# A two-layer decoder on one Trainium2 core: the last attention's value products turned round, with softmax sums on VectorE

## The chip, the cores and the metric

The kernel runs on one core of a Trainium2 chip. The metric is the device time of one execution in microseconds (us): lower is better. The core has a matrix engine (TensorE, in the profile PE, its weight loads PEld), a vector engine (VectorE, DVE), a scalar engine (ScalarE, ACT), a general engine (GpSimd, POOL) and a queue engine that here only issues transfers (SyncE, SP). Matrix products land in PSUM, eight banks of 128 partitions by 512 float32; everything else is in SBUF or in DRAM.

## The reference, cut to what matters

A batch of 32 sequences of 56 tokens with 128 features goes through two post-norm layers. Each has self-mixing, cross attention on a context of 1500 rows by 128 features per sequence, and a mixture of eight experts. The change touches the cross attention of layer 1:

```
q  = layernorm(x) @ w_q               # 16 heads of 64
k, v = split(context @ w_kv)          # 16 heads of 64
scores = einsum('bqhd,bkhd->bhqk', q * 64**-0.5, k)
attn = softmax(scores, axis=-1)       # over 1500 context rows
out = einsum('bhqk,bkhd->bqhd', attn, v)
return (out @ w_out + b_out) * tanh(gate)
```

The kernel folds the key projection into the queries and the value projection into the output weights, so that scores and values are both products with the context itself: for each sequence there are 16 x 56 = 896 query columns of 128 features.

## The kernel before, in words

All arithmetic is float32. The work of layer 1's cross attention is written by the generator `attention()` (L1059). It goes over 64 blocks: for each of the 32 sequences one of 512 query columns and one of 384 (`BLOCKS`). The 1500 context rows are cut into 12 chunks (`CK`) of 125 rows (`PK`). A pass of its loop writes three things that overlap:

- the scores of the current block `cur`. For each chunk, one product (L1077) of the transposed context `amT` (stationary, 128x125) with the queries (moving, 128x512 or 128x384) into one of three banks of pool `p_s`, which ACT copies to the SBUF tile `s` (L1078). DVE keeps a running maximum of the chunks in `m` (L1083 to L1087).
- the values of the block before, `prev`. For each 128 query columns, 12 products (L1182) of the probabilities (stationary, 125x128) with the context rows `amN` (moving, 125x129) into one of two banks of pool `p_v`. The 129th column of `amN` is one, so the last column of the bank is the sum of the probabilities. DVE takes its reciprocal `rz` (L1189), and ACT scales the bank by it into `ao` (L1191).
- the outputs of the block before that, `old`: TensorE transposes each `ao` tile into a bank, and DVE copies it into `qo` (L1199). `outputs` stands at chunk 5 of the next score loop.

Between them stand `maxima` (TensorE transposes `m`, DVE reduces), `spread` (the negated maxima transposed back into rows, `nb`, copied by ACT at L1163), and the four parts of `probabilities` (DVE adds `nb` to three chunks, L1171; ACT takes the exponential, L1174). Some of those parts are still due when the next score loop begins.

At every `yield` of `attention()` a hand-written planner (L1279 to L1306) writes steps of two other threads into the program: `pre` (layer 0 and the first half of layer 1 for later sequences) and `post` (output projection and experts of finished sequences). Their matmuls use pool `p_f`. How many steps it writes follows from the product count of `attention()` so far, so filler and attention keep pace. The framework then decides the order on each queue: it may move a ready instruction past one that stands earlier in the code. In the profile, for example, the copy L1199, written behind a maximum at chunk 5, runs ahead of it.

All transfers are issued from SP before the change. The opening works on the first two groups of sequences in step: loads of weights, of `xin` (L967) and of contexts, then `self_attention` with the transposes of x as its first product. `obias`, a small product and an addition (L396), stands ahead of it.

Of the kernel before, what the change touches and what calls it, by code (L numbers as in the profile page):

```python
# [69 lines left out]
def decoder_kernel(  # L70
# [86 lines left out]
        clock["pe"] += TRANSPOSE  # L157


    ident = const.tile([P, P], F32, name="ident")  # L160
    make_identity(nc, ident)

    sq = const.tile([P, N_SQ], F32, name="sq")
    nc.sync.dma_start(sq[:, : 4 * D], sq_w[:, : 4 * D])
    vec = const.tile([P, N_VEC], F32, name="vec")
    nc.sync.dma_start(vec, vecs)
    row = const.tile([P, N_ROW], F32, name="row")
    nc.sync.dma_start(row, rows.to_broadcast([P, N_ROW]))
    svec = const.tile([SD, len(SVEC)], F32, name="svec")
# [18 lines left out]
    qo = [const.tile([P, 2, NQ], F32, name=f"qo{i}") for i in range(3)]  # L188

    qpad0 = const.tile([P, G, 64], F32, name="qpad")  # L190
    nc.gpsimd.memset(qpad0, 0.0)
# [14 lines left out]
    def vcol(name):  # L206
        i = VEC.index(name)
        return vec[:, i : i + 1]
# [180 lines left out]
    def ahead(a, b, tag="res", bufs=2):  # L389
# [3 lines left out]


    obias = const.tile([TP, D], F32, name="obias")
    nc.vector.tensor_tensor(  # L396
        obias, linear(vcol("bv0").to_broadcast([P, TP]), sqw("wo0"), D, TP), rowb("bo0"), ALU.add
    )

# [15 lines left out]
    def self_attention(xs):  # L415
# [8 lines left out]
            .unsqueeze(2).to_broadcast([P, nb, 2, S]),  # L424
        )
        xT = xd[:, :, 0, :]
        res = [ahead(t, obias) for t in xs]
        yield HOP
        qpad = here(qpad0, "qpad")[:, :nb]
# [565 lines left out]
    early = {}  # L995

    def opening(g):
        xs = load_x(g)
        load_x0(GROUPS[g][0])
        yield 0  # L1000
        xs = yield from self_attention(xs)
        xs = yield from cross_attention_0(xs, g)
        if g == 0:
            load_attended_T(0)
            acc = yield from experts_0(xs)
            early["weights"] = True
            yield from behind_experts(acc, g)
            return
        load_attended(0)
        while "weights" not in early:  # L1010
            yield None
        acc = yield from experts_0(xs)

        while not leader.over:
            yield None
        place["aside"] = None
        early["acc"] = []
        for a in acc:
            t = tok_tile("acc")
            nc.gpsimd.tensor_copy(t, a)  # L1020
            early["acc"].append(t)
# [34 lines left out]

    def attention():  # L1059
        blocks = [(b, q0, n) for b in range(B) for q0, n in BLOCKS]  # L1060
        prev = None
# [1 line left out]
        tail = []  # L1063
        for i in range(len(blocks) + 2):
            cur = None
            if i < len(blocks):
                b, q0, n = blocks[i]
                if q0 == 0:
# [6 lines left out]
                for c in range(CK):  # L1075
                    ps = bank(p_s, "s")
                    mm(ps[:PK, :n], amT[:, c * PK : (c + 1) * PK], qT)  # L1077
                    nc.scalar.copy(s[:, c, :], ps[:PK, :n])  # L1078


                    if c % 2 == 1 and 1 < c < CK - 2:
                        a = s[:, 0:2, :] if c == 3 else m
                        nc.vector.tensor_tensor(m, a, s[:, c - 1 : c + 1, :], ALU.max)  # L1083
                        if c == CK - 3:
                            nc.vector.tensor_tensor(m[:, 0, :], m[:, 0, :], m[:, 1, :], ALU.max)  # L1085
                    elif c >= CK - 2:
                        nc.vector.tensor_tensor(m[:, 0, :], m[:, 0, :], s[:, c, :], ALU.max)  # L1087
                    if c % 2 == 0 and tail:
                        tail.pop(0)()
                    if not tail:  # L1090
                        table["gelu"] = True
                    if c == 5 and old is not None:
                        outputs(old)
                        old = None
                    if c % 2:
                        yield 0
                if q0 and b + 1 < B:
                    load_attended_T(b + 1)
            elif old is not None:
                outputs(old)  # L1100
                old = None
            for f in tail:
                f()
            tail = []
            os = []
            nt = prev[2] // P if prev else 0
            for t in range(max(nt, 2)):
                if t < nt:
                    po = values(prev, t)
                    for k in range(3):  # L1110
                        next(po)
                        if t == 1 and k == 1 and cur:
                            table["gelu"] = False
                            nb = spread(cur, nm)
                            tail = probabilities(cur, nb)
                            for f in tail[:1]:
                                f()
                            tail = tail[1:]
                        yield 0
                    os.append(next(po))  # L1120
                elif t == 1 and cur:
                    yield 1.0
                    nb = spread(cur, nm)
                    tail = probabilities(cur, nb)
                if t == 0 and cur:
                    if not nt:
                        yield 1.0
                    nm = maxima(cur, m)
                if t >= 2 and tail:
                    tail.pop(0)()  # L1130
            if prev:
                old = (prev, os)
# [23 lines left out]
    def spread(blk, nm):  # L1156

        n = blk[2]
        ps = bank(p_t, "t")
        for t in range(n // P):  # L1160
            tr(ps[:PK, t * P : (t + 1) * P], nm[:, t : t + 1].to_broadcast([P, PK]))
        nb = mid.tile([PK, 512], F32, tag="nb", name="nb")[:, :n]
        nc.scalar.copy(nb, ps[:PK, :n])  # L1163
        return nb

# [9 lines left out]

        return [lambda k=k: part(k) for k in range(4)]

    def values(blk, t):
        b, _, _, s = blk
        po = bank(p_v, "v")  # L1180
        for c in range(CK):
            mm(  # L1182
                po[:, : D + 1], s[:, c, t * P : (t + 1) * P], amN[b % 2][:, c, :],
                start=(c == 0), stop=(c == CK - 1),
            )
            if c % 4 == 3:
                yield
        rz = tiny.tile([P, 1], F32, tag="rz1", name="rz1")
        nc.vector.reciprocal(rz, po[:, D : D + 1])  # L1189
        o = work.tile([P, D], F32, tag="ao", name="ao", bufs=5)  # L1190
        nc.scalar.activation(o, po[:, :D], AF.Copy, scale=rz)  # L1191
        yield o

    def outputs(old):
        (b, q0, n, _), os = old
        ps = bank(p_t, "t")
        for t, o in enumerate(os):
            tr(ps[:, t * P : (t + 1) * P], o)
        nc.vector.tensor_copy(qo[(b // 2) % 3][:, b % 2, q0 : q0 + n], ps[:, :n])  # L1199
        if q0 and b % 2:  # L1200
            attended.add(b // 2)

# [193 lines left out]
```

## Time and profile before

| | |
|---|---|
| median of three runs | 2210.01 us (2209.82 to 2216.82) |
| the profiled execution | 2217.4 us, its span 2215.7 us |
| PE busy | 2146.1 us, 97% of the span |
| DVE busy | 1436.4 us, 65% |
| ACT busy | 1208.6 us, 55% |
| POOL busy | 142.5 us, 6% |
| mean granted TensorE clock | 0.992 |
| mean transfer rate | 78 GB/s |

A line of a group reads: line, engine, operation, output<-inputs, shapes, how many | busy us, mean ns of one | how long the engine stood idle just before them and who ended that. PE busy is not the same as PE cost: matmuls are pipelined, so the duration of one overlaps the next. What a product costs in a stream is the distance from its start to the next one's start. Each float32 product is two matmul instructions in the trace.

### The profile page before, as it was taken

Reading aid. Unit: us, or ns where it says so; the run is one execution under the profiler, and the core shown is the slowest. Engines: PE = TensorE matmul, PEld = TensorE weight load, DVE = VectorE, ACT = ScalarE, POOL = GpSimd, SP = SyncE. Lnnn points to the kernel's source line nnn. Section 1 sums busy time; section 2 is a strip of 40 time slices with the busy share of each in tenths; the row PEclk is TensorE's granted clock in tenths of the full one; section 3 lists DMA queues with packets and bytes.
Section 4 is the critical chain, followed back from the end, with each engine's and each line's share of the span. In section 5 each row is a group of like instructions: output and inputs, shape, how many; then the busy total and the mean of one; then the engine's idle time right before and its main releaser. Section 6 shows DMA issues by size and latency. Waiting matters only on the chain.

```text
span 2215.7 us, 36884 instructions
## 1 busy us (share of the span) xinstructions
PE 2146.1 (97%) x14560; PEld 1706.4 (77%) x14560; DVE 1436.4 (65%) x2981; ACT 1208.6 (55%) x2165; POOL 142.5 (6%) x230
## 2 busy tenths in 40 slices
PE   7799999999999999999999999999999999999997
PEld 5677778778877787777877878777887878878876
DVE  4367655866577656766577765777567766667774
ACT  2455575556455556556555555555465556565551
POOL 2000001100010000100010000100001000000000
PEclk9899999999999999999999999999999999999998
DMA  7621431143211522124320343113331132111221
GB/s 200 179 81 31 112 71 62 51 125 85 75 31 57 133 84 73 31 77 116 90 64 17 93 117 97 41 30 111 102 90 29 57 106 81 43 42 50 60 79 37
DMA packets 164300, 172.17 MB, mean 78 GB/s; under 512 B 9464, under 2 KB 136864, under 8 KB 164000
## 3 DMA queue, kind: packets, MB, share of 16 engines
q1 hardware_dynamic: 164128, 169.82, 27.5%
q8 instruction: 115, 1.88, 0.4%
q14 instruction: 57, 0.47, 0.1%
HBM read 144.29 MB, written 25.49 MB: 77 GB/s over the span
## 4 chain that ended last, share of the span: by engine, by line
PE 68%; DVE 9%; ACT 3%; POOL 2%; issue 1%; DMA 1%; POOLq 0%; SPq 0%; ACTq 0%; DVEq 0%
PE f L147 25%; PE s L147 20%; PE v L147 18%; DVE s L1171 4%; PE f L156 3%; PE t L156 3%; POOL rs L360 2%; DVE m L1083 1%; ACT s L1174 1%; DVE m L1087 1%; ACT nb L1163 0%; ACT s L1078 0%; DVE st L351 0%; DMA memT<-big 0%; DVE m L1085 0%
## 5 line engine op out<-in xcount | busy, mean ns | idle before, releaser
L147 PE MATMUL v<-amN,s 125*128 125x129 f32 x5376 | 695.4, 276 | 0.9 <-ACT s L1174 0.5
L147 PEld LDWEIGHTS v<-amN,s 125*128 125x128 f32 x5376 | 655.5, 191 | 36.1 <-issue 23.5
L147 PE MATMUL s<-qo,amT 128*125 128x512 f32 (+1 forms) x1536 | 648.1, 543 | 1.9 <-ACT s L1078 1.9
L1078 ACT COPY s<-s 125x512 f32<-125x512 f32 (+1 forms) x768 | 399.7, 538 | 267.7 <-PE s L147 265.0
L1171 DVE TENSOR_TENSOR s<-s,nb 125x1536 f32<-125x1536 f32 (+1 forms) x256 | 392.9, 1545 | 59.2 <-ACT nb L1163 58.7
L147 PEld LDWEIGHTS s<-qo,amT 128*125 128x125 f32 x1536 | 264.1, 188 | 162.9 <-issue 95.2
L1174 ACT ACTIVATE s<-s 125x1536 f32<-125x1536 f32 (+1 forms) x256 | 339.1, 1328 | 85.4 <-DVE s L1171 79.9
L1083 DVE TENSOR_TENSOR m<-m,s 125x1024 f32<-125x1024 f32 (+1 forms) x192 | 208.8, 1088 | 67.6 <-ACT s L1078 65.6
L360 POOL TENSOR_TENSOR rs<-rs,mhalf 112x1 f32<-112x1 f32 x126 | 81.9, 661 | 1702.9 <-DVE rs L359 1456.0
L1191 ACT ACTIVATE ao<-v,rz 128x128 f32<-128x128 f32 x224 | 81.0, 363 | 163.8 <-DVE rz L1189 163.6
L753 ACT ACTIVATE hT<-f,vec 128x224 f32<-128x224 f32 (+1 forms) x256 | 95.3, 435 | 73.8 <-PE f L147 73.3
L147 PEld LDWEIGHTS f<-wd,hT 128*112 128x112 f32 x960 | 114.7, 180 | 16.7 <-ACT hT L753 7.3
L147 PE MATMUL f<-wd,hT 128*112 128x128 f32 x960 | 124.3, 279 | 1.7 <-ACT hT L753 1.4
L147 PE MATMUL f<-pxT,w 128*128 128x224 f32 (+1 forms) x576 | 118.1, 344 | 3.1 <-DMA w<-in_up_dram 1.4
L147 PE MATMUL f<-xT,wu 128*128 128x224 f32 (+1 forms) x512 | 110.3, 351 | 7.6 <-DMA wu<-in_wup_dram 6.4
L147 PEld LDWEIGHTS f<-pxT,w 128*128 128x128 f32 x576 | 99.0, 194 | 20.1 <-issue 4.2
L147 PEld LDWEIGHTS f<-xT,wu 128*128 128x128 f32 x512 | 90.6, 194 | 24.7 <-issue 13.2
L1083 DVE TENSOR_TENSOR m<-s 125x1024 f32<-125x1024 f32 x64 | 69.5, 1086 | 61.4 <-ACT s L1078 61.1
L771 DVE SCALAR_TENSOR_TENSOR acc<-f,wmix,acc 112x128 f32<-112x128 f32 x120 | 41.1, 347 | 86.9 <-PE f L147 86.8
L1163 ACT COPY nb<-t 125x512 f32<-125x512 f32 x64 | 34.0, 532 | 111.1 <-PE t L156 111.1
L1087 DVE TENSOR_TENSOR m<-m,s 125x384 f32<-125x384 f32 (+1 forms) x128 | 80.3, 628 | 21.2 <-ACT s L1078 14.9
L147 PE MATMUL f<-w,h 128*112 128x128 f32 x512 | 78.7, 276 | 1.6 <-DVE th L936 1.6
(289 smaller groups left out, 2376.1 us busy)
## 6 DMA issues: line engine op xcount, KB each, us to landing
amT<-memT SPq DMA_DIRECT2D x32, 750.0 KB
amN<-in_mem_dram SPq DMA_DIRECT2D x34, 672.0 KB
memT<-big SPq DMA_DIRECT2D x30, 750.0 KB
cxN<-in_mem_dram SPq DMA_DIRECT2D x30, 672.0 KB
wu<-in_wup_dram SPq DMA_DIRECT2D x72, 256.0 KB
wd<-in_wdn_dram SPq DMA_DIRECT2D x72, 256.0 KB
w<-in_gate_dram SPq DMA_DIRECT2D x72, 128.0 KB
w<-in_up_dram SPq DMA_DIRECT2D x72, 128.0 KB
```

The lines of the kernel that those rows point to most:

```text
L147: nc.tensor.matmul(ps, lhsT=lhsT, rhs=rhs, start=start, stop=stop)
L156: nc.tensor.transpose(ps, in_, ident[:k, :k])
L360: nc.gpsimd.tensor_tensor(rs, rs, mhalf[:TP], ALU.pow)
L753: nc.scalar.activation(hT[:, u0 + k, :], ps[:, k * nt : (k + 1) * nt], AF.Gelu, bias=vec[:, c : c + 1],)
L771: nc.vector.scalar_tensor_tensor(acc[j], down(last[1], last[0][1], nu, j), w[:, j, e - 1 : e], acc[j], ALU.mult, ALU.add,)
L1078: nc.scalar.copy(s[:, c, :], ps[:PK, :n])
L1083: nc.vector.tensor_tensor(m, a, s[:, c - 1 : c + 1, :], ALU.max)
L1087: nc.vector.tensor_tensor(m[:, 0, :], m[:, 0, :], s[:, c, :], ALU.max)
L1163: nc.scalar.copy(nb, ps[:PK, :n])
L1171: nc.vector.tensor_tensor(c, c, nb.unsqueeze(1).to_broadcast([PK, 3, n]), ALU.add)
L1174: nc.scalar.activation(c, c, AF.Exp)
L1191: nc.scalar.activation(o, po[:, :D], AF.Copy, scale=rz)
```

## The change

In layer 1's value products the context chunk (125x128) is now stationary and the block's probabilities (125x512 or 125x384) move, so a block takes 12 products instead of 48 or 36, and the result already has features on partitions. No transpose of an `ao` tile remains. The sums of the probabilities no longer come from a column of ones. DVE adds the chunks in pairs, five additions a block (`chunk_sums`, at chunks 2 to 10 of the next score loop). At chunk 1 of the score loop after that, eight small products with a 125x32 tile of ones finish the sums into four quarters of a `p_v` bank, and DVE takes reciprocals (`inverse_sums`). At chunk 4, ACT's queue stores one row of each quarter to DRAM (`store_sums`); at chunk 8 it loads them back, repeated on all 128 partitions (`spread_sums`); at chunk 11, DVE multiplies the value bank by them into `qo` (`outputs`). The bank of the values is held until then. The loop over values yields 12 times for every block. `maxima`, `spread` and the parts of `probabilities` move to chunks 2, 4, 8 and 11 of it.

In the opening, the first two x tiles are loaded from ACT's queue ahead of everything else, into a part of `qo`; `vecs` is loaded ahead of the first part of `sq`; and `obias` is made behind the first copy of the transposed x.

```diff
+    qo = [const.tile([P, 2, NQ], F32, name=f"qo{i}") for i in range(3)]
+    x_first = [qo[i][:TP, 0, :D] for i in range(2)]
+    for i, t in enumerate(x_first):
+        nc.scalar.dma_start(t, x[i * TP : (i + 1) * TP, :])
     ident = const.tile([P, P], F32, name="ident")
     make_identity(nc, ident)
     sq = const.tile([P, N_SQ], F32, name="sq")
-    nc.sync.dma_start(sq[:, : 4 * D], sq_w[:, : 4 * D])
     vec = const.tile([P, N_VEC], F32, name="vec")
     nc.sync.dma_start(vec, vecs)
+    nc.sync.dma_start(sq[:, : 4 * D], sq_w[:, : 4 * D])
...
+    ones = const.tile([PK, 32], F32, name="ones")
+    nc.gpsimd.memset(ones, 1.0)
...
         xT = xd[:, :, 0, :]
+        if not made:
+            make_obias()
+            made.append(True)
...
     def opening(g):
-        xs = load_x(g)
+        xs = [x_first[g]]
...
             cur = None
+            adds = chunk_sums(prev) if prev else []
...
-                    if c == 5 and old is not None:
-                        outputs(old)
-                        old = None
+                    if adds and c in (2, 4, 6, 8, 10):
+                        adds.pop(0)()
+                    if old is not None:
+                        if c == 1:
+                            old = (*old, inverse_sums(old))
+                        elif c == 4:
+                            old = (*old, store_sums(old))
+                        elif c == 8:
+                            old = (*old, spread_sums(old))
+                        elif c == CK - 1:
+                            outputs(old)
+                            old = None
...
+            if prev:
+                po = bank(p_v, "v")
+            for c in range(CK):
+                if prev:
+                    value_chunk(prev, po, c)
+                if cur and c == 2:
...
+                    nm = maxima(cur, m)
+                if cur and c == 4:
...
+                    tail.pop(0)()
+                if tail and prev and (c == 8 or c == CK - 1 and prev[2] == 512):
+                    tail.pop(0)()
+                if prev:
+                    yield 0
...
-    def values(blk, t):
...
+    def chunk_sums(blk):
+        _, _, n, s = blk
+        f = mid.tile([P, 2, 512], F32, tag="zf", name="zf")[:PK, :, :n]
+        def add(c):
+            nc.vector.tensor_tensor(
+                f, s[:, 0:2, :] if c == 2 else f, s[:, c : c + 2, :], ALU.add
+            )
+        sums[0] = f
+        return [lambda c=c: add(c) for c in range(2, CK, 2)]
+    def inverse_sums(old):
+        n, f = old[0][2] // 4, old[2]
+        ps = bank(p_v, "v")
+        for g in range(4):
+            for k in range(2):
+                mm(
+                    ps[32 * g : 32 * g + 32, :n], ones, f[:, k, g * n : (g + 1) * n],
+                    start=(k == 0), stop=(k == 1),
+                )
+        rz = work.tile([P, P], F32, tag="rz1", name="rz1", bufs=1)[:, :n]
+        nc.vector.reciprocal(rz, ps[:, :n])
+        return rz
+    def value_chunk(blk, po, c):
+        b, _, n, s = blk
+        mm(po[:, :n], amN[b % 2][:, c, :D], s[:, c, :], start=(c == 0), stop=(c == CK - 1))
+    def store_sums(old):
+        n = old[0][2] // 4
+        zd = dram.tile([4, P], F32, tag="zd", name="zd", bufs=4)[:, :n]
+        nc.scalar.dma_start(zd, old[3].rearrange("(g r) n -> g r n", g=4)[:, 0, :])
+        return zd
+    def spread_sums(old):
+        n = old[0][2]
+        rzb = mid.tile([P, 512], F32, tag="nb", name="rzb")[:, :n]
+        nc.scalar.dma_start(
+            rzb.rearrange("p (g n) -> p g n", g=4),
+            old[4].unsqueeze(0).to_broadcast([P, 4, n // 4]),
+        )
+        return rzb
     def outputs(old):
-        (b, q0, n, _), os = old
-        ps = bank(p_t, "t")
-        for t, o in enumerate(os):
-            tr(ps[:, t * P : (t + 1) * P], o)
-        nc.vector.tensor_copy(qo[(b // 2) % 3][:, b % 2, q0 : q0 + n], ps[:, :n])
+        (b, q0, n, _), po, *_, rzb = old
+        nc.vector.tensor_tensor(
+            qo[(b // 2) % 3][:, b % 2, q0 : q0 + n], po[:, :n], rzb[:, :n], ALU.mult
+        )
```

More of the change, by code (lines that the diff above doesn't have):

```diff
@@ L186, in decoder_kernel @@
     memT = [dram.tile([P, CK * PK], F32, tag=f"memT{b}", name=f"memT{b}") for b in range(B)]
-    qo = [const.tile([P, 2, NQ], F32, name=f"qo{i}") for i in range(3)]
+    ones = const.tile([PK, 32], F32, name="ones")
+    nc.gpsimd.memset(ones, 1.0)
     qpad0 = const.tile([P, G, 64], F32, name="qpad")
@@ L395, in decoder_kernel, with make_obias @@
     obias = const.tile([TP, D], F32, name="obias")
-    nc.vector.tensor_tensor(
-        obias, linear(vcol("bv0").to_broadcast([P, TP]), sqw("wo0"), D, TP), rowb("bo0"), ALU.add
-    )
+    made = []
+    def make_obias():
+        nc.vector.tensor_tensor(
+            obias, linear(vcol("bv0").to_broadcast([P, TP]), sqw("wo0"), D, TP), rowb("bo0"), ALU.add
+        )
     HOP, NORM, LOAD = 2.5, 6.0, 14.0
@@ L1099, in attention @@
             elif old is not None:
-                outputs(old)
+                old = (*old, inverse_sums(old))
+                old = (*old, store_sums(old))
+                outputs((*old, spread_sums(old)))
                 old = None
-            for f in tail:
+            for f in tail + adds:
                 f()
             tail = []
[L1105 to L1122, printed above, removed]
+            if prev:
[4 more added lines that the diff above has]
+                if cur and c == 2:
+                    if not prev:
+                        yield 1.0
+                    nm = maxima(cur, m)
+                if cur and c == 4:
+                    if not prev:
+                        yield 1.0
+                    table["gelu"] = False
                     nb = spread(cur, nm)
                     tail = probabilities(cur, nb)
[L1125 to L1129, printed above, removed]
                     tail.pop(0)()
+                if tail and prev and (c == 8 or c == CK - 1 and prev[2] == 512):
+                    tail.pop(0)()
+                if prev:
+                    yield 0
             if prev:
-                old = (prev, os)
+                old = (prev, po, sums[0])
             if cur and cur[1] == 0 and cur[0] + 1 < B:
@@ L1161, in spread @@
             tr(ps[:PK, t * P : (t + 1) * P], nm[:, t : t + 1].to_broadcast([P, PK]))
-        nb = mid.tile([PK, 512], F32, tag="nb", name="nb")[:, :n]
+        nb = mid.tile([P, 512], F32, tag="nb", name="nb")[:PK, :n]
         nc.scalar.copy(nb, ps[:PK, :n])
@@ L1176, in probabilities @@
         return [lambda k=k: part(k) for k in range(4)]
-    def values(blk, t):
[L1179 to L1184, printed above, removed]
-            )
[L1186 to L1192, printed above, removed]
@@ new lines, in decoder_kernel @@
+    sums = [None]
+    def inverse_sums(old):
[13 more added lines that the diff above has]
+        mm(po[:, :n], amN[b % 2][:, c, :D], s[:, c, :], start=(c == 0), stop=(c == CK - 1))
@@ L1200, in outputs @@
+    def outputs(old):
+        (b, q0, n, _), po, *_, rzb = old
+        nc.vector.tensor_tensor(
+            qo[(b // 2) % 3][:, b % 2, q0 : q0 + n], po[:, :n], rzb[:, :n], ALU.mult
+        )
         if q0 and b % 2:
```

## The prediction

> **What bounds the kernel now.** I read the page first: busy time, then the releasers of the engines, then the chain, then the groups by shape.
>
> ```profile
> PE 2146.1 (97%) x14560; PEld 1706.4 (77%) x14560; DVE 1436.4 (65%) x2981; ACT 1208.6 (55%) x2165; POOL 142.5 (6%) x230
> ```
>
> PE is busy 97% of the span. Busy alone would not prove a bound, so the waits of PE come next (engine and line, who ended the wait, total us, times, longest):
>
> ```profile
> PE t L156 <- DVE rz L1189: 7.7, 6, 1.7
> ...
> PE t L156 <- DVE m L1087: 4.5, 7, 1.4
> ...
> PE s L147 <- ACT s L1078: 1.9, 4, 1.0
> ...
> PE v L147 <- ACT s L1174: 0.5, 1, 0.5
> ```
>
> No other engine holds PE up in the attention: a few us in 2200. So time moves by what TensorE has to stream, and by any wait the change puts there. What a product costs is read from the chain of waits (start, us, what), in one stretch where the two kinds follow each other:
>
> ```profile
> 917.16 2.57 PE s L147 x6
> 919.73 0.44 PE f L147 x4
> 920.17 2.68 PE v L147 x24
> ```
>
> A score matmul (512 moving columns) takes 2.57/6 = 0.43 us; a value matmul (129 columns) 2.68/24 = 0.112 us. Four of the latter make 0.447 us: in an unbroken stream the two shapes are 4% apart. The groups by shape give the counts and the prices of the rest:
>
> ```profile
> L147 PE MATMUL v<-amN,s 125*128 125x129 f32 x5376 | 695.4, 276 | 0.9 <-ACT s L1174 0.5 <-ACT ao L1191 0.3
> L147 PE MATMUL s<-qo,amT 128*125 128x512 f32 x768 | 361.9, 594 | 1.3 <-ACT s L1078 1.3
> L147 PE MATMUL s<-qo,amT 128*125 128x384 f32 x768 | 286.4, 493 | 0.6 <-ACT s L1078 0.5
> L1083 DVE TENSOR_TENSOR m<-m,s 125x1024 f32<-125x1024 f32 x96 | 117.1, 1219 | 35.4 <-ACT s L1078 35.4
> L1083 DVE TENSOR_TENSOR m<-m,s 125x768 f32<-125x768 f32 x96 | 91.8, 956 | 32.2 <-ACT s L1078 30.3
> L1191 ACT ACTIVATE ao<-v,rz 128x128 f32<-128x128 f32 x224 | 81.0, 363 | 163.8 <-DVE rz L1189 163.6
> L156 PE MATMUL t<-ident,ao 128*128 128x128 f32 x224 | 39.0, 276 | 0.3 <-ACT ao L1191 0.2
> L1189 DVE RECIPROCAL rz<-v 128x1 f32<-128x1 f32 x224 | 35.8, 160 | 50.7 <-PE v L147 50.4
> L534 DVE RECIPROCAL o<-f 128x112 f32<-128x112 f32 x15 | 12.8, 853 | 11.5 <-PE f L147 11.4
> ```
>
> **The change part by part**
>
> *Value products.* Because durations overlap, I count in the trace's records each matmul from its start to the next matmul's start. The 5376 value matmuls sum to 644.5 us; their median is 112 ns, so 42 us of it is what the first of each run costs more (about 0.1 us when other work has stood before it). The new form has the shape of the scores: 12 products, two matmuls each, of 512 or 384 columns, 768 matmuls of each width. The score rows counted the same way are 335.5 and 259.3 us, together 594.8 us. Minus 50 us, all on the path.
>
> *Transposes of ao.* 224 at 109 ns plus their switches, 26.9 us from start to start. Gone: minus 27 us.
>
> *Sums on TensorE.* Eight products of 125x32 with 128 (or 96) columns a block, 16 matmuls. The nearest row is self-attention's sum with vmask (112x32, 128 columns), where 16 matmuls over four column groups take 0.46 us, and about 0.1 us more is lost on entering and on leaving: 0.66 us, or about 0.55 us with 96 columns, 39 us in 64 blocks. There, however, neighbours lie in different column groups; here the two products of one group follow each other. The Trainium skill ("TensorE: Matmul & The Clock Gate", Part 3, What overlaps and what doesn't) says that matmuls start and end in program order without overtaking. By that rule, four matmuls of one group run one after another and only the last of a group overlaps the first of the next: 13 slots of 0.107 us, 1.6 and 1.25 us a block with the switches, 91 us in all, and the gain on TensorE is spent. The row speaks against so strict an order: in it the first halves of four products start 7 ns apart, the second halves 0.1 us later. I take 45 us, close to the row, and keep 39 and 91.
>
> *DVE.* Five additions a block have the shape of L1083: 5 x (1.219 + 0.956) x 32 = 348 us. A reciprocal of 128x128 or 128x96 at L534's 7.6 ns a column is 0.97 or 0.73 us: 54 us. The product in outputs replaces a copy of the same size from PSUM (0.69 us), for nothing. The small reciprocals go: minus 36. DVE comes to about 1802 us, 81%. What hides it: no value product needs the additions of its own block, which have a whole value loop and a score loop to be done in. Three stages of two blocks in a row (score, value, score; columns: us, then busy us of PE, PEld, DVE, ACT, POOL, clock, share and rate of the transfers):
>
> ```profile
> 905.90:919.60 13.70, 13.70 (x48) 7.79 (x48) 7.60 (x10) 8.41 (x17) 2.18 (x2) 1.00 0.03 9
> 919.60:935.00 15.40, 15.28 (x174) 12.61 (x173) 13.49 (x27) 5.91 (x11) 0.00 (x0) 1.00 0.01 1
> 935.00:951.80 16.80, 16.74 (x137) 12.26 (x136) 12.11 (x19) 10.67 (x18) 0.11 (x1) 1.00 0.21 47
> ```
>
> Over all such stages of the steady part, a pair of blocks lasts 65.3 us and DVE is busy for 43.4 of them; the additions, reciprocals and saved instructions make that about 55. There is room, but the framework must spread it: a score stage that gets all five additions and the reciprocal is close to full (10.2 of 17.0 us on average with 512 columns, plus 4.8 and 1.0). If that cover is gone, what runs late first is the multiplication in outputs, behind which the value bank hangs.
>
> *The way of the reciprocals.* Product with ones 0.66, reciprocal 0.97, store, load, multiplication 0.69 us. The trace shows no such small store in the steady part; its bounds come from the opening. The 24 KB load of vec, issued at 1.25 us, ended a wait at 3.92: 2.7 us. The load of row is the very shape of the new one (one DRAM row of 260 KB in all, repeated on 128 partitions): issued at 1.72, it ended waits at 5.73, 4.0 us, under full traffic. With 0.4 and 0.8 us for the two issues the chain is 10.2 us. Four queues take a turn in it, each behind whatever they are doing, so about 13. From chunk 1 to the end a score stage offers 15 us on average (17.0 and 16.4 us less two chunks), but the stages vary by 4.5 us, and a bare one has only 11 x 0.86 = 9.5 or 11 x 0.65 = 7.1. When the reciprocals are late, the next block's first value product waits: pool p_v has two banks, one goes to the sums, and the other holds the old values until outputs has read them. Behind that product stands all of TensorE's queue. A lateness of max(0, 13 minus stage) would average about 1.1 us, 70 us in 64 blocks; fewer if ready filler takes its place. I take 15 us, bounds 0 and 100: below zero is excluded, since the bank was free before.
>
> *ACT.* The scalings of ao go, minus 81 us. Two transfers a block come, 128 issues at 0.36 to 1.1 us (the opening's), about as much. The store makes ACT wait for the reciprocal, and the load for the store's landing. Queued behind them are the score copies L1078, and TensorE can run three banks ahead of those, 2.6 or 1.9 us. At chunks 4 and 8 there should be enough distance. I cost it at nothing; without the cushion it is part of the same 0 to 100.
>
> *Moved steps.* maxima stood behind 24 value matmuls (2.7 us) and now stands behind three chunks (2.6 or 1.9); spread behind 40 (4.5 us), now five chunks (4.3 or 3.2). Nothing. The parts of probabilities keep their number on both sides of the seam.
>
> *Opening.*
>
> ```profile
> 5.73 0.20 ACT L268 ACTIVATE tgate<-row 128x1 f32<-128x1 f32 x1 [3.65 <-DMA row<-in_rows_dram]
> ...
> 7.43 0.42 PE L156 MATMUL f<-ident,xin 112*128 112x112 f32 x1 [2.77 <-DMA xin<-in_x_dram]
> ```
>
> x was issued at 4.40 us and used at 7.43. From ACT's queue at 0.8 it can be there at 3.8. The query product needs sq, which now lands one issue (0.44 us) later than 3.89. Its copy on ACT stands behind tgate and so comes at 5.9 instead of 9.2: 3.2 us earlier at most. SP loses two issues ahead of the contexts (0.9 us). obias moves on PE and DVE behind the first copy and waits there for row until 5.8; POOL's residual, which needs it, was made at 8.8 and is read at 24. But the transfers are 99% busy in the first 20 us, and what is loaded doesn't get less. Bounds 0 and minus 3.2, I take minus 2.
>
> **The sum.** -50 - 27 + 45 - 2 + 15 = -19 us. The profiled execution took 2217.4 us (span 2215.7); it becomes 2198. It stood 7.4 us above the median of the runs, 2210.0, so I predict 2191 for the median.
>
> **Rivals.**
>
> *Late reciprocals, slower.* The place is the first value product of each block, the mechanism the value bank held until DVE's multiplication. TensorE wins 50 + 27 - 45 + 2 = 34 us, so it decides from 34/64 = 0.53 us of lateness a block. At 1.5 us a block it costs 96 and the time is 2210 + 62 = 2272. For it: 13 us of chain in a stage that may be as short as 8 to 12, and DVE at 81%. Against it: the average stage is longer than the chain, and TensorE has filler.
>
> *The sums run one after another.* 91 for 45: 2210 - 50 - 27 + 91 - 2 + 15 = 2237. For it the rule; against it the row.
>
> *Full cover.* Sums at the row's 39, opening -3, no wait: 2210 - 41 = 2169. For it: TensorE waits for almost nothing today, and value products of 0.43 us hide their weight loads.
>
> *A draw.* 34 us of waits eat the gain: 2210.
>
> **How the numbers follow.** A measurement of this kernel can tell about 0.3%, 6.6 us. Chances: the sum as worked out 0.32 (its own range 2175 to 2203), full cover 0.18, draw 0.10, serial sums 0.14, late reciprocals 0.26. That is faster 0.50, same 0.10, slower 0.40. The range goes from below full cover (2158) into the late reciprocals (2268, 1.4 us a block), which leaves out the worst half of that case and the best of full cover.
>
> **What would show it.** Right: value matmuls 768 + 768 with a start-to-start sum near 595; no transposes of ao; 1024 matmuls with ones, 0.5 to 0.7 us for 16; DVE near 1800 us; PE's waits for DVE's outputs below 20 us. Wrong: the first value product of a block waiting 1 us or more for DVE or for the load of the reciprocals; ACT waiting at its two transfers with PE waiting for L1078; ones products 0.1 us apart.

## The result, and the profile after

The changed kernel takes 2270.33 us in the median of 4 runs (2267.9 to 2274.76), against 2210.87 for the kernel before on the same chip: a ratio of 1.0266 (95% interval 1.0241 to 1.029). The forecast was 2191, range 2158 to 2268, with faster the likelier sign. It was wrong in sign, and the measured time lies 2 us outside the range. The profiled execution took 2274.8 us, its span is 2273.0.

The engines, on the page of the changed kernel:

```profile
PE 2174.3 (96%) x11520; PEld 1383.3 (61%) x11520; DVE 1745.6 (77%) x3141; ACT 1153.5 (51%) x1953; POOL 144.2 (6%) x231
```

PE has 3040 fewer instructions and is busy 28 us longer. Durations overlap, so its busy time says little of what the products cost, and part of the 28 us is a lower clock (below). The groups by shape of the same kernel say what the products cost and what DVE gained:

```profile
L147 PE MATMUL v<-s,amN 125*128 125x512 f32 x768 | 364.9, 598 | 4.1 <-ACT s L1198 1.7 <-DVE mv L361 1.1 <-issue 1.1
L147 PE MATMUL v<-s,amN 125*128 125x384 f32 x768 | 284.9, 497 | 9.1 <-DVE rz L1226 6.5 <-DVE rs L367 2.3 <-DVE m L684 0.3
L1207 DVE TENSOR_TENSOR zf<-zf,s 125x1024 f32<-125x1024 f32 x128 | 155.9, 1218 | 2.7 <-ACT s L1198 2.2
L1207 DVE TENSOR_TENSOR zf<-zf,s 125x768 f32<-125x768 f32 x128 | 122.0, 953 | 2.0
L1226 DVE RECIPROCAL rz<-v 128x128 f32<-128x128 f32 x32 | 30.4, 950 | 15.5 <-PE v L147 15.4
L1250 DVE TENSOR_TENSOR qo<-v,rzb 128x512 f32<-128x512 f32 x32 | 21.9, 683 | 6.2 <-DMA rzb<-zd 6.2
```

The value products have the scores' durations (598 and 497 ns a matmul against 594 and 493), the additions 1.218 and 0.953 us, the reciprocal 0.95, the multiplication 0.683: the prices of the prediction hold. From start to start the value matmuls sum to 611.6 us (644.5 before), their medians 429 and 323 ns exactly those of the scores. The timeline, in one value stage (start, duration, engine, what; in brackets how long it waited and for whom), shows the new products, one wait, the products behind it (those up to 922.5 at half their pace, see below), and the products with ones:

```profile
917.45 0.91 PE L147 MATMUL v<-s,amN 125*128 125x384 f32 x2 [2.46 <-DVE rz L1226]
...
918.86 5.19 PE L147 MATMUL v<-s,amN 125*128 125x384 f32 x10
...
924.32 3.39 PE L147 MATMUL v<-s,amN 125*128 125x384 f32 x10
...
928.84 0.56 PE L147 MATMUL v<-zf,ones 125*32 125x96 f32 x16
```

In the first line TensorE stands still for 2.5 us until the reciprocal has read a value bank. This is near the wait that the rival *late reciprocals* named, but another instruction of DVE ends it: the rival had the first value product wait for the multiplication in `outputs`. But the waits of PE over the whole span (engine and line, who ended it, total, times, longest) show how little of it there is:

```profile
PE f L156 <- DVE h L373: 7.3, 11, 1.3
PE f L147 <- DVE xT L812: 7.2, 2, 3.8
...
PE v L147 <- DVE rz L1226: 6.5, 4, 2.5
...
PE s L147 <- ACT s L1097: 3.6, 4, 1.9
```

Four waits at the value products, 6.5 us, cannot be the 60. The longest rows stand at tile `f`, behind `h` and `xT`: work of the filler, not of attention. So the next question is where filler waits with nothing beside it. The value stage behind the scores of 384 columns lasted 17.9 us before, with a deviation of 3.6; now it lasts 20.4, with a deviation of 9.8. Every eighth block is the cause. Here are two of these stages (the last block of a group of four sequences), of the kernel before (columns as in the prediction: us, then busy us of PE, PEld, DVE, ACT, POOL, clock, transfers):

```profile
887.30:905.90 18.60, 16.66 (x111) 15.74 (x110) 12.33 (x32) 8.67 (x17) 4.79 (x8) 0.91 0.13 42
1155.40:1172.70 17.30, 15.29 (x112) 14.24 (x111) 12.13 (x32) 8.55 (x17) 4.79 (x8) 1.00 0.14 45
...
sum 138.30, PE 127.31 PEld 119.02 DVE 95.21 ACT 67.21 POOL 29.01; mean PE 18.19 PEld 17.00 DVE 13.60 ACT 9.60 POOL 4.14
```

and of the changed one:

```profile
900.00:934.90 34.90, 30.68 (x127) 16.49 (x126) 27.73 (x55) 9.92 (x18) 3.88 (x8) 0.95 0.19 53
1171.50:1204.40 32.90, 29.75 (x129) 16.05 (x128) 27.06 (x64) 9.79 (x19) 6.31 (x12) 1.00 0.21 55
...
sum 252.40, PE 215.75 PEld 126.67 DVE 182.79 ACT 78.70 POOL 39.77; mean PE 30.82 PEld 18.10 DVE 26.11 ACT 11.24 POOL 5.68
```

The sum lines are over all seven such stages: 138 us have become 252, and the time in them in which PE is not busy has gone from 11.0 to 36.7 us. Most of the 114 us is work that has only moved. The scores of the next block need the new group's queries and stand behind its preparation, and the value products of the next value stage go ahead of them. The products of 384 columns in the timeline above are such products, and that next stage shrinks, in six of the seven to 0.6 us or less (8 to 17 us before). So the fair stretch is the long stage and the two behind it, from the last score product before it to the first of the next 384 columns. The sums over all seven, before and after:

```profile
sum 321.54, PE 309.49 PEld 243.04 DVE 225.90 ACT 158.15 POOL 43.48; mean PE 44.21 PEld 34.72 DVE 32.27 ACT 22.59 POOL 6.21
sum 343.12, PE 306.47 PEld 174.25 DVE 229.74 ACT 135.68 POOL 41.60; mean PE 43.78 PEld 24.89 DVE 32.82 ACT 19.38 POOL 5.94
```

That is 22 us more, and PE not busy for 36.7 us in place of 12.1. The long stages end where a new group of sequences enters layer 1. Before the planner lets it enter, it writes what is left of that group's preparation in one go (`finish()`), and that is a chain of small products, DVE and POOL steps that wait for one another.

The planner finds out how far attention has come from `main.spent / PAIR_US`: the product count of `attention()` so far, divided by what a pair of sequences is supposed to cost, a constant of 80.5 us. The change makes attention cheaper by that count (worked out from the program's own cost formula: 1304.1 us for all pairs before, 1265.9 after) and leaves the constant as it is. So the planner thinks that attention has come less far than it has, and holds filler back. When a group must enter, this much of the 70.9 us of its preparation has been written (counted in the program; first to seventh time): before 63.9, 67.0, 68.6, 68.6, 70.9, all, all; after 63.7, 64.4, 64.4, 63.7, 62.7, 62.7, 62.4. What is held back is also missing at the end: from the last value product to the last product of all it is 31.8 us before and 44.7 after (in both profiles, PE starts).

The profile shows one thing more that nobody had priced, the granted clock. In the kernel before it is halved (0.50) in 6 stretches, in the changed one in 13. The sums over these stretches, before and after:

```profile
sum 37.32, PE 32.43 PEld 29.07 DVE 12.81 ACT 9.02 POOL 0.70; mean PE 5.40 PEld 4.84 DVE 2.13 ACT 1.50 POOL 0.12
sum 80.83, PE 70.13 PEld 50.22 DVE 37.83 ACT 20.57 POOL 7.11; mean PE 5.39 PEld 3.86 DVE 2.91 ACT 1.58 POOL 0.55
```

One of the 13 is 919.0 to 922.5, in the timeline above: there the value matmuls of 384 columns start 0.64 us apart, and 0.32 once it is over. In 12 of the 13, PE had been idle for at least 1.4 of the 3.4 us before; the one at 1792.9 follows no idle time. PE is busy at half clock for 38 us more than before, so up to half of that, 19 us, passes through the clock (an estimate, at most; no run separates it).

### The profile page after: what moved, and what is told of

It reads as the page before. It is cut to its first block, busy times and chain, and to the rows that moved or that the text cites. A ratio compares the mean times of both kernels' runs of the same rounds, so it can differ in the third digit from the quotient of the medians.

```text
span 2273.0 us, 31014 instructions
## 1 busy us (share of the span) xinstructions
PE 2174.3 (96%) x11520; PEld 1383.3 (61%) x11520; DVE 1745.6 (77%) x3141; ACT 1153.5 (51%) x1953; POOL 144.2 (6%) x231
## 4 chain that ended last, share of the span: by engine, by line
PE 66%; DVE 11%; ACT 2%; issue 2%; POOL 2%; DMA 1%; POOLq 0%; DVEq 0%; ACTq 0%
PE f L147 24%; PE v L147 19%; PE s L147 18%; DVE s L1195 3%; PE f L156 3%; POOL rs L368 2%; PE t L156 2%; DVE m L1102 1%; DVE zf L1207 1%; ACT s L1198 1%; DVE rz L1226 1%; DVE m L1106 1%; DVE st L359 0%; DMA w<-in_gate_dram 0%; DVE y L373 0%
## 5 line engine op out<-in xcount | busy, mean ns | idle before, releaser
L147 PE MATMUL v<-s,amN 125*128 125x512 f32 (+1 forms) x1536 | 649.8, 547 | 13.2 <-DVE rz L1226 6.5
L147 PE MATMUL s<-qo,amT 128*125 128x512 f32 (+1 forms) x1536 | 655.6, 548 | 3.6 <-ACT s L1097 3.6
L147 PEld LDWEIGHTS v<-s,amN 125*128 125x128 f32 x1536 | 274.7, 192 | 198.5 <-issue 115.4
L147 PEld LDWEIGHTS s<-qo,amT 128*125 128x125 f32 x1536 | 267.7, 188 | 188.5 <-issue 109.4
L1207 DVE TENSOR_TENSOR zf<-zf,s 125x1024 f32<-125x1024 f32 (+1 forms) x256 | 278.0, 1086 | 4.7 <-ACT s L1198 2.2
L368 POOL TENSOR_TENSOR rs<-rs,mhalf 112x1 f32<-112x1 f32 x126 | 85.7, 692 | 1771.0 <-DVE rs L367 1601.1
L147 PEld LDWEIGHTS f<-wd,hT 128*112 128x112 f32 x960 | 116.7, 180 | 26.7 <-issue 7.7
L147 PE MATMUL f<-pxT,w 128*128 128x224 f32 (+1 forms) x576 | 120.7, 346 | 6.0 <-DVE h L954 1.4
L147 PE MATMUL f<-wd,hT 128*112 128x128 f32 x960 | 124.4, 279 | 2.1 <-ACT hT L768 0.9
L147 PEld LDWEIGHTS f<-pxT,w 128*128 128x128 f32 x576 | 99.1, 194 | 32.6 <-DVE h L954 5.7
L147 PE MATMUL f<-xT,wu 128*128 128x224 f32 (+1 forms) x512 | 110.8, 352 | 8.1 <-DMA wu<-in_wup_dram 6.9
L147 PEld LDWEIGHTS f<-xT,wu 128*128 128x128 f32 x512 | 91.9, 195 | 29.9 <-issue 14.6
L950 ACT ACTIVATE th<-f 128x448 f32<-128x448 f32 (+1 forms) x81 | 40.5, 500 | 103.2 <-PE f L147 89.9
L147 PEld LDWEIGHTS f<-w,h 128*112 128x112 f32 x512 | 68.3, 178 | 33.5 <-issue 11.1
```

What stands on the lines that cost most here:

```text
L147: nc.tensor.matmul(ps, lhsT=lhsT, rhs=rhs, start=start, stop=stop)
L368: nc.gpsimd.tensor_tensor(rs, rs, mhalf[:TP], ALU.pow)
L950: nc.scalar.activation(th, pg[:, : nu * n], AF.Tanh, scale=0.5)
L1207: nc.vector.tensor_tensor(f, s[:, 0:2, :] if c == 2 else f, s[:, c : c + 2, :], ALU.add)
```

## The experiments

Each run is compared with the kernel before on its own chip, whose median moved between 2210 and 2216. So differences are taken from ratios: 1% is 22.1 us. All kernels but two start from the changed one, the two from the kernel before. The first theory was that waits behind the reciprocals eat the gain (the late reciprocals of the prediction); the rivals that came up were the load of DVE and the planner's pace.

**e1: the value products alone.** It leaves out the whole normalisation: no additions, no products with ones, no reciprocals, no transfers; the value bank is copied at chunk 5.

```diff
-            adds = chunk_sums(prev) if prev else []
+            adds = []
...
-        nc.vector.tensor_tensor(
-            qo[(b // 2) % 3][:, b % 2, q0 : q0 + n], po[:, :n], rzb[:, :n], ALU.mult
-        )
+        nc.vector.tensor_copy(qo[(b // 2) % 3][:, b % 2, q0 : q0 + n], po[:, :n])
```

> The changed kernel without any normalisation: no chunk additions, no ones products, no reciprocals, no transfers; outputs copies the value bank into qo at chunk 5 of the score loop (left out: the division by the sums). It holds the turned value products and the opening alone. All theories: TensorE keeps the 50 + 27 us, so about 2210 - 77 - 3 = 2130 us; if value products with the context stationary do not pay on their own (mis-sized term), 2180 or more.

Measured: 2194.92 us, ratio 0.9927 [0.9905, 0.995]. With no normalisation at all, only 16 us of some 80 are gained. So the other 63 us or so were lost to something that is not the normalisation, or were never there to gain. This is the miss that led to the planner: without the products with ones attention is cheaper still (1236.4 us by the count), and only 51 to 64 us of a group's 70.9 are written when it must enter.

**e2, e3, e4: one suspected wait at a time, constant as it was.** e2 makes one addition a block in place of five (it leaves out eight chunks of the sums):

```diff
-        return [lambda c=c: add(c) for c in range(2, CK, 2)]
+        return [lambda c=c: add(c) for c in range(2, 4, 2)]
```

> The changed kernel with one chunk addition a block instead of five (left out: eight of the twelve chunks in the sums). Takes 4/5 of L1207's 348 us off VectorE and leaves bank, ones products, reciprocals and transfers. Theory VectorE's load (the additions make everything that TensorE's filler waits for late): back by 60 us or more, to 2200 or below. Theory held bank or transfers (the first value product waits for the reciprocals' way): hardly a change, 2255 to 2270.

e3 takes the bank of the sums from the pool of the transposes, so that the value banks are not used for them:

```diff
-        ps = bank(p_v, "v")
+        ps = bank(p_t, "t")
```

> The changed kernel with the ones products in pool p_t instead of p_v, so that the two p_v banks alternate between blocks and the first value product of a block no longer waits for outputs. Nothing is left out. Theory held bank: back by 50 us or more, to 2220 or below. Theory VectorE's load: 2255 to 2275.

e4 leaves out the load of the reciprocals and with it the division: the old values are multiplied by a row that lies in SBUF.

```diff
-        rzb = mid.tile([P, 512], F32, tag="nb", name="rzb")[:, :n]
-        nc.scalar.dma_start(...)
-        return rzb
+        return row[:, :n]
```

> The changed kernel without the load of the reciprocals from DRAM: outputs multiplies by a constant tile (left out: the division by the sums; sums, reciprocals and the store stay). Theory late reciprocals: the bank comes free without the trip, 2220 or below. Theory VectorE's load: 2255 to 2275.

Measured: e2 2260.55, 1.0236 [1.0203, 1.0269]; e3 2263.67, 1.0238 [1.0211, 1.0265]; e4 2264.17, 1.0228 [1.0202, 1.0255]. Each gives 6 to 8 us against 1.0266, with intervals that touch that of the changed kernel. None of the three is where the 59 us went, taken one by one under the wrong pace.

**e5, e6, e10: the pace.** The constant is the only edit of e5, scaled as the product count fell. The count of written preparation at each entry is then within 1 us that of the kernel before (63.7, 67.8, 68.6, 68.6, 70.1, all, all):

```diff
-PRE_US, POST_US, PAIR_US = 71.3, 31.0, 80.5
+PRE_US, POST_US, PAIR_US = 71.3, 31.0, 78.1
```

> The changed kernel with PAIR_US 78.1 in place of 80.5, nothing else. The planner's count of attention work fell from 1304 to 1266 us by its own costs, while the divisor that turns it into pairs stayed, so filler is written too slowly; at each need of a new pair 6.5 to 8.5 us of the pre thread (0 to 7 before, mostly 2) is written in one go, without attention work between. 78.1 = 80.5 x 1266/1304. Theory pace: back by 25 us or more, to 2245 or below. Theory that the reciprocals' path and the ones products alone cost it: no change, 2262 to 2275.

e6 is e1 with the constant at 76.3. It leaves out what e1 leaves out.

> Values alone without normalisation (as e1: the division by the sums is left out) with PAIR_US 76.3 = 80.5 x 1236/1304. Theory pace: the turned value products then give what the sum said, 2130 to 2150 us, against 2195 of e1. If the value products themselves are mis-sized: 2180 or more.

e10 is the counterproof: the kernel before with 82.9, which makes its planner as late as the changed kernel's (the same seven counts, to 0.3 us).

> The kernel before, with nothing but PAIR_US 82.9 (80.5 x 1304/1266), which slows its planner as the change slowed its own. Theory pace: 20 to 35 us slower than before, about 2240, as e5 gained 29. If pace hurts only with the turned value products: within 8 us of before.

Measured: e5 2241.13, 1.0118 [1.0099, 1.0136]; e6 2150.88, 0.9708 [0.9691, 0.9725]; e10 2231.55, 1.0077 [1.0053, 1.0101]. The constant alone is worth 33 us to the changed kernel (1.0266 to 1.0118) and 48 us to e1 (0.9927 to 0.9708). In the kernel before, the same lateness costs 17 us, 3 below the range expected of it: the effect is there, and half as large, so the changed kernel suffers more from the same lateness than the old one. The profiles say where. In e10 attention takes no longer than before (2022 us for 2023 from the first score product to the last), and it is the end behind it that grows (74 for 59). The changed kernel has, against e5, 27 us more in attention (2067 for 2041) and 10 at the end (75 for 65). Two of the stages of the table above, now of e5:

```profile
904.20:920.10 15.90, 14.21 (x68) 8.40 (x66) 13.84 (x33) 6.44 (x11) 4.63 (x8) 1.00 0.15 50
1171.10:1189.50 18.40, 16.62 (x78) 10.25 (x77) 16.40 (x36) 7.43 (x12) 4.31 (x8) 1.00 0.13 42
```

34.9 and 32.9 us have gone back to 15.9 and 18.4; only the first of the seven stays at 44, as the count at its entry stays at 63.7. With the two stages behind them the seven take 318 us, for 343. The clock is not what the constant repairs: it was 0.985 in the median of the changed kernel's runs and 0.984 in e5's. What the changed kernel loses at the right pace is still 26 us, and between e5 and e6 lie 90: the price of the normalisation. The other runs take it apart, all at the right pace.

**e7, e8, e11: bank and additions.** e7 is e5 with the edit of e3, e8 is e5 with that of e2, e11 has both.

> The changed kernel with PAIR_US 78.1 and the ones products in pool p_t, so that the value banks alternate (nothing left out). Theory held bank, hidden so far under the planner's bunches: 20 us or more below e5. Otherwise within 10 us of e5.

> The changed kernel with PAIR_US 78.1 and one chunk addition a block instead of five (left out: eight of twelve chunks in the sums). Theory VectorE's load, hidden so far under the planner's bunches: 20 us or more below e5. Otherwise within 10 us of e5.

> The changed kernel with PAIR_US 78.1, the ones products in pool p_t and one chunk addition a block instead of five (left out: eight of twelve chunks in the sums). Tells whether held bank and additions are separate costs: 2185 to 2192 if they add up (2241 - 27 - 26), 2205 to 2215 if they are one.

Measured: e7 2214.33, 0.9997 [0.9985, 1.0009]; e8 2214.89, 1.0007 [0.9996, 1.0019]; e11 2206.48, 0.9964 [0.9951, 0.9976]. The bank alone is worth 27 us, the additions alone 25, both together 34. So most of it is one cost that either edit takes away. The reading that fits is the value bank that the sums borrow, which comes free late because DVE, with the additions, comes late (from the reciprocal's start to the multiplication's 12.8 us in the median of e5, 8.7 in e8). With the bank out of the way, four fifths of the additions are worth 7 us. The direct wait for it is gone from the waits of PE in e7, where value products wait only for their own probabilities:

```profile
PE v L147 <- ACT s L1198: 7.3, 6, 2.5
PE v L147 <- DVE m L301: 0.4, 2, 0.2
```

In e5 the line `PE v L147 <- DVE rz L1226` stood at 3.4 us. So the 27 us are mostly not in that line. They are waits all the same: PE's waits for DVE sum to 39.9 us in e5 and 31.2 in e7, those for ACT to 22.5 and 14.4, and the whole time in which PE is not busy falls from 88.2 to 71.1, 17 of the 20 us between these two profiled executions. By which steps a late bank reaches the other tiles is not shown.

**e9: the additions on GpSimd.** e7 with `nc.gpsimd.tensor_tensor` for the five additions.

> The changed kernel with PAIR_US 78.1, the ones products in pool p_t, and the five chunk additions a block on GpSimd instead of VectorE (nothing left out). e7 and e8 each took 26 us off e5's 2241. If these two are separate costs and GpSimd's additions stay hidden, 2185 to 2195, faster than the kernel before. If they are one cost, about 2214. If GpSimd's additions slow VectorE or hold up its square roots for the filler, above 2214.

Measured: 2526.95, 1.1412 [1.1389, 1.1435]. The groups of e9:

```profile
L1207 POOL TENSOR_TENSOR zf<-zf,s 125x1024 f32<-125x1024 f32 x128 | 355.1, 2774 | 16.4 <-ACT s L1198 6.8
...
L1102 DVE TENSOR_TENSOR m<-m,s 125x768 f32<-125x768 f32 x96 | 184.8, 1925 | 27.9 <-ACT s L1097 25.8
```

against the same maximum in e7:

```profile
L1102 DVE TENSOR_TENSOR m<-m,s 125x768 f32<-125x768 f32 x96 | 91.3, 951 | 2.2 <-ACT s L1097 1.9
```

An addition takes 2.77 us in place of 1.22. The maxima of 768 columns that overlap one (63 of the 96) take 2.58 us in the median, the other 33 take 0.96, as in e7. POOL is 36% busy, so its share alone doesn't explain 14%; the small steps of layer norm that POOL makes for the filler (`rs`, L368) now stand behind additions of 2 to 3 us. PE is not busy for 277 us, 71 in e7, and the granted clock is 0.943, 0.988 in e7. How the 14% divide among these is not shown.

**e12: the opening alone**, on the kernel before: the two loads of x from ACT's queue, the order of `vecs` and `sq`, and the later `obias`, as in the diff of the change.

> The kernel before with the opening's edits alone: x from ScalarE's queue, vecs ahead of sq, obias behind the first copy. The prediction's term: 2 us faster, between 0 and 3.2. A static order shifted by the edit could hide it or make it up to 5 us slower.

Measured: 0.9989 [0.998, 0.9998], 2.4 us faster.

**e14, e15, e13: the rest.** e14 leaves out the sum over the partitions: no products with ones, and the reciprocal is taken of the added chunk itself. Its constant is 76.3, since attention is as much cheaper.

```diff
-        ps = bank(p_v, "v")
-        for g in range(4):
-            for k in range(2):
-                mm(...)
...
-        nc.vector.reciprocal(rz, ps[:, :n])
+        nc.vector.reciprocal(rz[:PK], f[:, 0, :n])
```

> Leaves out the sum over the partitions: no products with ones, the reciprocal is taken of the added chunk itself; additions, store, load and multiplication stay. PAIR_US 76.3 as in the values-alone kernel. The 90 us between values alone (2151) and the whole change at the right pace (2241) are the sum of: products with ones, bank, additions, and the rest (store, load, reciprocal, multiplication). Theory: ones 40 to 45 us and the bank's hold, which goes with them, 10 to 25: 2175 to 2190. Rival: it is the trip by way of DRAM and its users that hold TensorE: 2215 or more.

e15 is e7 with the edit of e4.

> Leaves out the division (the old values are multiplied by a row of biases that lies in SBUF): no load of the reciprocals; PAIR_US 78.1 and the sums' bank in p_t; the store, the reciprocal, additions and products with ones stay. Theory: the load's trip is hidden once the value banks are free, within 5 us of 2214 (ratio 0.998 to 1.002). Rival: the wait for the load still holds outputs and with it TensorE: 2200 or less (ratio 0.994).

e13 leaves nothing out. It is e7 with one addition more, which folds the two halves of the sums, and so with four products with ones a block in place of eight:

```diff
-PRE_US, POST_US, PAIR_US = 71.3, 31.0, 80.5
+PRE_US, POST_US, PAIR_US = 71.3, 31.0, 77.2
...
-                    if adds and c in (2, 4, 6, 8, 10):
+                    if adds and c in (2, 4, 6, 8, 10, 11):
...
+        def last():
+            nc.vector.tensor_tensor(f[:, 0, :], f[:, 0, :], f[:, 1, :], ALU.add)
...
-        ps = bank(p_v, "v")
+        ps = bank(p_t, "t")
         for g in range(4):
-            for k in range(2):
-                mm(...)
+            mm(ps[32 * g : 32 * g + 32, :n], ones, f[:, 0, g * n : (g + 1) * n])
```

> Nothing left out. PAIR_US 77.2 (the product count with half the ones products), the sums' bank in p_t, and one more addition on VectorE at chunk 11 (f[:,0] += f[:,1]), so that four products with ones a block are left instead of eight. If the time of the products with ones counts on TensorE: they go from 44 us to about 27 start to start, so about 2214 - 15 = 2200 (ratio 0.993). If VectorE's load is what now holds TensorE back: 39 us more of additions late in the score stage cost at least what they save, 2214 or more (ratio 1.0 or above).

Measured: e14 2191.44, 0.9884 [0.987, 0.9898]; e15 2204.76, 0.9946 [0.9933, 0.996]; e13 2202.53, 0.9934 [0.992, 0.9948]. e14, by its ratio 2184 us, lies within what the theory gave: products with ones and the bank that they hold are 52 us together, 27 of them the bank. e15 falls between its two theories, nearer to the rival: the load still costs 11 us where the banks are free. The edit also frees the SBUF buffers that the loaded rows share with `nb`, and the two were not tried apart. e13 comes out as expected if TensorE's time counts: 14 us less than e7, though DVE has more to do (1770 us busy for 1743):

```profile
PE 2128.9 (97%) x11008; PEld 1359.7 (62%) x11008; DVE 1770.0 (80%) x3205; ACT 1140.9 (52%) x1947; POOL 173.9 (8%) x231
```

e13 is the one complete kernel that is faster than both, by 0.66% than the kernel before. The three repairs (pace, bank, half of the ones products) turn 59 us of loss into 15 of gain.

## Why the prediction was wrong, step by step

The runs give a ladder, each step a difference of two ratios, in us of 2210:

| step | runs | us | predicted |
|---|---|---|---|
| value products, transposes, opening; no normalisation | before to e6 | -64.5 | -79 |
| additions, reciprocal, store, load, multiplication | e6 to e14 | +39 | in the 15 for waits |
| products with ones, without their bank | e14 to e5, less e5 to e7 | +25 | +45 |
| the value bank they hold | e7 to e5 | +27 | in the 15 for waits |
| the planner's pace | e5 to after | +33 | not priced |
| sum | before to after | +59 | -19 (with +15 for waits) |

The size of a step depends on the others: under the wrong pace the bank is worth 6 us (e3) and not 27, and the pace is worth 48 us without the normalisation (e1 to e6) and not 33.

- **Value products, -50, and transposes, -27.** The mechanism and the price per product were right (429 and 323 ns, and 611.6 us in all for 594.8). The term was some 15 us too large: in e6, without a normalisation, the value matmuls still take 606.2 us from start to start. The median is the scores' own, so 11 us of it lie where a run of them begins or ends: in e6 the sum stands 28 us above the medians, 7 of it at the first matmul of a run and 21 at the last, before other work starts. I had taken the scores' sum, with the scores' own breaks, for it. The prediction's reading of the old products has the same flaw: of the 42 us above their median, 33 stand at the last matmul of a run and 8 at the first. What the rest is stays open; the clock of e6's runs, 0.987 in the median for 0.993 before, is a candidate that was not tried.
- **Ones, +45.** The choice between row and rule was right. 16 matmuls take 0.595 us with 128 columns and 0.488 with 96, near the 0.66 and 0.55 of the row with vmask. The Trainium skill ("TensorE: Matmul & The Clock Gate", Part 3, What overlaps and what doesn't) states that matmuls start and end in order. The 13 slots one behind the other, which gave 1.6 and 1.25 us a block, were my own conclusion from it; the measured times refute them, and the rival built on them falls. The starts come in four lots of four, 13 ns apart inside a lot and 110 (with 96 columns 83) from lot to lot. The records don't name the column groups, so whether a lot is one group or all four is open. Taking half of them out gave 14 us (e7 to e13), so all of them are worth 25 to 28 by the runs, less than the 45. From start to start they do sum to 44.1 us in e7, so the price was right; that part of it lies in gaps that TensorE has anyway is argued.
- **Waits, +15.** This is the first step that failed. It stood for late reciprocals, the load by way of DRAM and ACT's blocking, with bounds 0 and 100, and was set near the lower bound because stages are longer on average than the chain. Together with the additions, costed at nothing, it measured 66 us (39 + 27), within the bounds that I gave it. The place was right, the value banks that DVE frees, and it is the rival's. The path was wrong: in the profile no wait of a value product ends with the multiplication in `outputs`; what costs is the bank lent to the sums, and the only wait at the value products that shows it is for `rz`, 6.5 us. That this rival's 2272 us, worked out for 1.5 us of lateness a block, stands next to the measured 2270 is luck: 33 of the 59 us are the planner's pace. From the reciprocal to the multiplication it is 13.2 us in the median of 64 blocks, and up to 47 (starts).
- **Additions, nothing.** Right only with a free bank (7 us for four of five, e7 to e11), wrong where the sums borrow a value bank (25 at the right pace, e5 to e8). DVE came to 1746 us, 77%, in place of 1802.
- **The planner, not priced.** This is the second step that failed, and it was there to be read: the text ahead of the prediction says that filler follows the product count of attention. The change moves that count by 38 us, and I did not ask what the constant beside it assumes. With it the planner falls behind, and that measured 33 us (e5 to after). The pace does not decide the sign: at the right pace (e5) the change still loses 26 us, against a forecast of 19 gained.
- **Moved steps, nothing; opening, -2.** The opening is shown (-2.4, e12). The first score product comes 3.4 us earlier in the changed kernel (130.5 for 133.9). The moved steps were not tried alone. The timeline of the changed kernel's opening shows the first product at 2.91 us for 7.43. It is still x that holds it: the last of its transfer lands at 2.78 us, and the identity has been made at 1.80. (The profile names the mask `lower`, which POOL had just finished and this product does not read.) The gate of row is where it was:

```profile
2.91 0.42 PE L156 MATMUL f<-ident,qo 112*128 112x112 f32 x1 [2.91 <-POOL lower L243]
...
5.68 0.20 ACT L276 ACTIVATE tgate<-row 128x1 f32<-128x1 f32 x1 [2.66 <-DMA row<-in_rows_dram]
```

- **ACT, nothing.** e15 gives the load 11 us, with its wait for the store. It could not be told apart whether ACT's blocking or the late multiplication makes them. The blocking that the prediction feared is there where the sums borrow a value bank: score copies wait behind the store (who waited, for whom, us, times, longest), here in the changed kernel, 13.0 us in three waits in e5, and never in e7.

```profile
ACT s L1097 <- DMA zd<-rz: 7.5, 2, 4.0
```

Of the 39 us between e6 and e14, 7 are the additions (e7 to e11) and 11 the load (e7 to e15), if these differences can be carried over. What the other 20 are stays open: the reciprocal, the store, and the later time of the multiplication (chunk 11 for 5) were not tried one by one.

The forecast of what would show it wrong, a first value product that waits 1 us or more, came true in four blocks at most. A better sign would have been the time in which PE is not busy, stage by stage, and not the waits at the products that the change touches.

## What to carry to other kernels

Where filler is written by a planner with a cost constant, a change that makes the main work cheaper also slows the planner down: set the constant anew before judging the change, and price it in a forecast (here 33 us, more than half of the loss). Look for the loss where TensorE stands still longer, not only where the new instructions stand: the waits of value products for `rz` were a tenth of it. And when a stage got longer, look at its neighbours before calling it a loss: here 114 us more in seven stages were 22 with the stages behind them. A scratch result that borrows a bank of a double-buffered pool takes the double buffer away (27 us by one changed pool, at the right pace), and an engine whose load was harmless before can become a bound through it.

## What the runs showed of the hardware

An elementwise addition of two SBUF operands on GpSimd slows VectorE's maxima beside it. In e9 those of 125x768 that overlap an addition take 2583 ns in the median (63 of them) and the others 957 (33); those of 125x1024 take 2303 (38) and 1219 (58). The addition itself takes 2.77 us for VectorE's 1.22. The Trainium skill ("SBUF — State Buffer", SBUF: two separate sides) has VectorE's instructions with two SBUF inputs and GpSimd share a pair of ports that one of them locks for a whole instruction; the numbers of e9 agree with that, though no run here shows that it is the ports.

A halved clock shows in the distance between matmuls. In the changed kernel's stretches with a granted clock of 0.50, value matmuls of 384 columns that follow each other start 640 ns apart in the median (10 of them), 323 over the whole run.
